# Probabilities turned on VectorE in 32-word squares instead of by transposing DMAs, and a causal mask added by products

## The chip, the cores and the metric

The kernel runs on one NeuronCore of one Trainium2 chip. Five engines work side by side from their own queues: TensorE (PE, with its weight loads PEld) multiplies matrices, VectorE (DVE) and ScalarE (ACT) work element by element, GpSimd (POOL) takes small side jobs and issues some DMAs, SyncE (SP) issues most DMAs. Sixteen DMA engines move the data. The metric is the device time of the program in microseconds (us); lower is better.

## The reference

One block of a transformer on a sequence of S = 2048 tokens of width 512: latent attention with 16 heads, a residual and a layer norm, then one linear layer, a residual and a layer norm.

```python
cq = rms_norm(x @ w_qa.T, q_a_ln_w)                       # 384 wide
q  = (cq @ w_qb.T) -> 16 heads of 128 (nope) + 64 (rope)
ckv = x @ w_kva.T                                         # 128 latent + 64 rope
kv = (rms_norm(ckv[..., :128], kv_a_ln_w) @ w_kvb.T) -> k_nope 128, v 128 per head
scores = (q_full @ k_full.T) * 192 ** -0.5
scores = where(causal, -inf, scores)
attn = softmax(scores)
out = (attn @ v) @ w_o.T
x = layernorm(x + out)
x = layernorm(x + x @ (weight * scale_weight[:, None]).T + bias)
```

## The kernel before

**Precision.** The products run at a precision of fp32 by splitting: a value is kept as a high and a low part (`split`, L61), and a product is the sum of high x high, high x low and low x high. The probabilities are split into two fp16 halves, and so are the latent values `V`.

**Absorbed weights.** The per-head key weights are multiplied into the query weights (L170), so that all 16 heads share one set of keys `Kn` (latent, 128 wide) and `Kp` (rope), and one set of values `V`. The value weights and the output weights are multiplied into `wvo` (L189), which acts on the attention's latent outputs at the end.

**Blocks and units.** The queries are four blocks `b` of 512. Within a block the loop runs over 8 pairs of heads `p` and four tiles `qt` of 128 queries. A *unit* is (b, p, qt): two heads `j`, each with nk = (4b + qt + 1) x 128 keys, so 128 to 512 in block 0 and 1664 to 2048 in block 3. Block 0 works on both heads at once (`pair_scores`, `pair_probs`), the others head by head (`head_scores`, `head_probs`).

**One head.** TensorE computes the scores into PSUM, five products per piece of up to 512 keys (L421). In the diagonal 128 columns the mask (-1e30 above the diagonal) is added: in block 0 and for the first head of a pair in block 3 by a sixth product, identity x mask (L423), elsewhere by VectorE on PSUM (L427). VectorE takes the maximum (L459) and forms the `bias` (L466, L468). ScalarE takes the exponentials and their sums (L474) into `pr`. VectorE forms `inv` (L484 to L487). ScalarE writes the high fp16 half of `pr * inv` (L495), VectorE the low half (L498), both into `hl`, high and low in separate rows. Then SP issues a transposing DMA (L502; L535 in block 0), which puts the keys on the partitions of the target: `PT` in block 0, a stretch of `ring` later.

**Order.** From block 1 on the instructions of TensorE and SP stand in the order in which the program writes them, in block 3 (from its second unit) those of VectorE and ScalarE too; the rest is ordered by a scheduler. `head_probs` of a head is a generator that `head_scores` of the next head drives, so the L498 of a head fall among the reductions of the next one, and its DMA behind the next head's `bias`. `values` (L540) multiplies the turned probabilities with `V` (L551), in two halves. `run_values(lag)` (L701) runs one half after each head once `lag` units wait; `lag` is 3 in blocks 1 and 2, and 2 in block 3, where the ring holds three units. So in block 3 the first half of unit n - 2 follows the scores of the first head of unit n. The result `ot` goes to DRAM by SP (`put_off` and `put_in`, L294 to L308). Projections of the next pair (`qn` L391, `pe` L347 to L376) are slipped in by `fill` (L562).

**Buffers.** In blocks 1, 2, 3 `hl` has 6, 4, 2 buffers and `pr` 4, 2, 2.

**Final stage.** Outputs come back from DRAM, are split (`latent`, L736) and multiplied with `wvo` into `acc` (`accumulate`, L766). `value_output` (L184) makes the `wvo` that are not there yet. Per tile of 128 tokens follow `residual`, `first_norm` and `ffn` (L867): transposes, split, GpSimd adds the bias to the residual (L874), 12 products (L880), VectorE adds both (L882), `layer_norm` (L847, whose root is two GpSimd instructions, L195 and L196), and one DMA out (L884).

Of the kernel before, what the change touches and what calls it, by code (L numbers as in the profile page):

```python
# [9 lines left out]
F16 = mybir.dt.float16  # L10
# [39 lines left out]
def mla_block(ctx: ExitStack, tc: tile.TileContext, a, out):  # L50
# [44 lines left out]

    ctx_kv = ctx.enter_context(ExitStack())
    kv = ctx_kv.enter_context(tc.tile_pool(name="kv", bufs=1))
    Kn = kv.tile([P, 2, S], F32R, name="Kn")
# [5 lines left out]
    with tc.tile_pool(name="ps_w", bufs=1, space=PSUM) as ps_w:  # L104
# [3 lines left out]
        for _ in range(10):  # L108
            nc.tensor.matmul(idle, ramp[:, :P], ramp, start=True, stop=True)

    blk = ctx.enter_context(tc.tile_pool(name="blk", bufs=2, side="right"))
    ctx_p = ctx.enter_context(ExitStack())
# [71 lines left out]
    def value_output(p, pool, tag):  # L184

        wvo = state["wvo"][p]
        for j in range(2):
            ps = pool.tile([P, HID], F32, tag=tag, name=f"ps_wo{2 * p + j}")
            nc.tensor.matmul(ps, state["wv"][:, 2 * p + j], state["wo"][2 * p + j], start=True, stop=True)  # L189
            split(ps, wvo[:, 0, j, :], wvo[:, 1, j, :], kvln_o)  # L190
            yield

    def rsqrt(dst, ms, n, eps):
        t = small.tile([P, 4], F32, tag="rs", name="rs_t")
        nc.gpsimd.tensor_scalar_add(t[:, :n], ms, eps)  # L195
        nc.gpsimd.tensor_tensor(dst, t[:, :n], nhalf[:, :n], ALU.pow)  # L196
# [212 lines left out]
    def score(ps, c0, w, b, p, j, qt, masked):  # L409

        qs = slice(qt * P, (qt + 1) * P)
        qn = state["qn", b, p]
        pe = state["pe", b, p // 2]
        qh, ql = qn[:, 0, j, qs], qn[:, 1, j, qs]
        qp = pe[:, 2 * (p % 2) + j, qs]

        by_product = b == 0 or b == 3 and j == 0
        ops = [(qh, Kn, 0), (qh, Kn, 1), (ql, Kn, 0), (qp, Kp, 0), (qp, Kp, 1)]
        n = 0
        for lhs, K, i in ops:  # L420
            nc.tensor.matmul(ps[:, :w], lhs, K[:, i, c0 : c0 + w], start=n == 0, stop=n == 4)  # L421
            if n == 1 and masked is not None and by_product:
                nc.tensor.matmul(ps[:, masked : masked + P], identb, maskb, start=False, stop=False)  # L423
            n += 1
        if masked is not None and not by_product:
            dg = ps[:, masked : masked + P]
            nc.vector.tensor_tensor(dg, dg, maskb, ALU.add)  # L427

# [3 lines left out]
    def head_scores(pools, b, p, j, qt, nk, prev):  # L432
# [36 lines left out]
        for _ in prev:  # L469
            pass  # L470
        pr = pools[1].tile([P, nk], F32, tag="pr", name=f"pr{b}_{p}_{qt}_{j}", bufs=4 if b == 1 else 2)
        sums = small.tile([P, 2], F32, tag="sums", name="sums")
# [15 lines left out]
        return pr, inv  # L488

    def head_probs(pools, b, p, j, qt, nk, PT, pr, inv):  # L490
        hl = pools[0].tile([P, 2, nk], F16, tag="hl", name=f"hl{b}_{p}_{qt}_{j}", bufs=(6, 4, 2)[b - 1])
        step = nk if nk <= 1024 else nk // 2
        cuts = [slice(c, c + step) for c in range(0, nk, step)]
        for c in cuts:
            nc.scalar.activation(hl[:, 0, c], pr[:, c], AF.Copy, scale=inv)  # L495
        yield
        for c in cuts:
            nc.vector.scalar_tensor_tensor(hl[:, 1, c], pr[:, c], inv, hl[:, 0, c], ALU.mult, ALU.subtract)  # L498
            if c != cuts[-1]:
                yield  # L500
        n2 = 2 * nk
        nc.sync.dma_start_transpose(  # L502
            PT[:, j * n2 : (j + 1) * n2].rearrange("p (k q) -> p k q", q=P), hl.rearrange("p a c -> p (a c)")
        )
        put_in()

    def pair_scores(pool, b, p, qt, nk):
# [3 lines left out]
        ps = psum["s"].tile([P, 2, 512], F32, tag="s", name=f"s{b}_{p}_{qt}")  # L511
        for j in range(2):
            score(ps[:, j, :], 0, w, b, p, j, qt, nk - P)
        neg = small.tile([P, 2], F32, tag="neg", name="neg")
# [14 lines left out]
    def pair_probs(pool, b, p, qt, nk, PT, pr, inv):  # L529
        hl = pool.tile([P, 2, 2, nk], F16, tag=f"hl{qt}", name=f"hl{b}_{p}_{qt}")  # L530
        for j in range(2):
            iv = inv[:, j : j + 1]
            nc.scalar.activation(hl[:, j, 0, :], pr[:, j, :], AF.Copy, scale=iv)
            nc.vector.scalar_tensor_tensor(hl[:, j, 1, :], pr[:, j, :], iv, hl[:, j, 0, :], ALU.mult, ALU.subtract)
        nc.sync.dma_start_transpose(  # L535
            PT[:, : 4 * nk].rearrange("p (k q) -> p k q", q=P), hl.rearrange("p j a c -> p (j a c)")
        )
        yield

    def values(b, p, qt, nk, PT):  # L540

        kts = nk // P
        v = PT[:, : 4 * nk].rearrange("p (j a k q) -> p j a k q", j=2, a=2, k=kts)
        ps = psum["m"].tile([P, 512], F32, tag="m", name=f"o{b}_{p}_{qt}")
# [296 lines left out]
    def load_fw(kt):  # L841
        raw = pc.tile([P, HID], F32, tag="xb", name=f"fraw{kt}", bufs=2)
        nc.scalar.dma_start(raw, a["fw"][:, kt])
        nc.vector.tensor_tensor(raw, raw, fsc, ALU.mult)
        split(raw, fw[:, 0, kt, :], fw[:, 1, kt, :])

    def layer_norm(dst, src):  # L847
        st = small.tile([P, 6], F32, tag="bn", name="bn")
        nc.vector.bn_stats(st, src)  # L849
        mv = small.tile([P, 2], F32, tag="mv", name="mv")  # L850
        nc.vector.bn_aggr(mv, st)
        r = small.tile([P, 1], F32, tag="lnr", name="lnr")
        rsqrt(r, mv[:, 1:2], 1, 1e-5)
        nc.vector.tensor_scalar(dst, src, mv[:, 0:1], r, ALU.subtract, ALU.mult)

# [11 lines left out]
    def ffn(t, x1):  # L867
# [5 lines left out]
        xb = pc.tile([P, HID], F32, tag="xb", name=f"xb{t}", bufs=2)  # L873
        nc.gpsimd.tensor_tensor(xb, x1, fb, ALU.add)  # L874
        yield 1
        ps = ps_f.tile([P, HID], F32, tag="ff", name=f"ff{t}")
        n = 0
        for kt in range(KT):
            for l, i in ((0, 0), (0, 1), (1, 0)):
                nc.tensor.matmul(ps, xt[:, l, kt, :], fw[:, i, kt, :], start=n == 0, stop=n == 11)  # L880
                n += 1
        nc.vector.tensor_tensor(xb, ps, xb, ALU.add)  # L882
        layer_norm(xb, xb)
        nc.sync.dma_start(out[0, t * P : (t + 1) * P, :], xb)  # L884

# [8 lines left out]
    with tc.manual_schedule(engines={ET.PE}):  # L894
        order = [(b, p) for b in range(NB) for p in range(NPAIR)]
        for b in range(NB):
            last = b == NB - 1
            if b:
                accs = [ps_a.tile([P, HID], F32, tag="acc", name=f"acc{b}_{t}") for t in range(4)]
            for p in range(0 if b else EARLY, CUT if last else NPAIR):  # L900
# [3 lines left out]
                for t in range(4):  # L904
                    accumulate(accs[t], p, t, *cuts[b, p])
                    if b == 0 and p + 2 < NPAIR and t == 1:
                        for _ in value_output(p + 2, ps_f, "ff"):
                            pass
                    if (p, t) in ((1, 2), (2, 0), (2, 2), (3, 0), (3, 2), (4, 0), (4, 2), (5, 0)):
                        advance()  # L910
# [76 lines left out]
```

## Time and profile before

| | us |
|---|---|
| median of 3 runs (lowest to highest) | 1588.22 (1586.73 to 1588.98) |
| the profiled execution, its time | 1588.17 |
| its span | 1586.40 |
| granted TensorE clock over the span | 0.993 |
| block 0's units, 52.2 to 253.6 of the span | 201.3 |
| block 1, 253.6 to 495.5 | 241.9 |
| block 2, 495.5 to 851.9 | 356.4 |
| block 3, 851.9 to 1331.7 | 479.8 |
| final stage, 1331.7 to 1586.4 | 254.7 |
| 192 transposing DMAs of blocks 1 to 3, issue to landing, median | 5.5 |

The span runs from the program's first profiled instruction to its last, and what lies around it is 1.77 us. A busy time is the time in which an engine has an instruction under way, and not a measure of how well it is used. In a group of instructions the columns are line, engine, operation, names of the output and the inputs, shapes, count, then busy us and the mean ns of one, then the idle time of the engine ahead of them and what ended it. A row of a timeline has start, length, engine, line, operation, names and the count of merged instructions; SPq is SP issuing a DMA. PE starts of successive products tell their pace, since the recorded lengths overlap.

### The profile page before, as it was taken

Reading aid. Unit: us, or ns where it says so; the run is one execution under the profiler, and the core shown is the slowest. Engines: PE = TensorE matmul, PEld = TensorE weight load, DVE = VectorE, ACT = ScalarE, POOL = GpSimd, SP = SyncE. Lnnn points to the kernel's source line nnn. Section 1 sums busy time; section 2 is a strip of 40 time slices with the busy share of each in tenths; the row PEclk is TensorE's granted clock in tenths of the full one; section 3 lists DMA queues with packets and bytes.
Section 4 is the critical chain, followed back from the end, with each engine's and each line's share of the span. In section 5 each row is a group of like instructions: output and inputs, shape, how many; then the busy total and the mean of one; then the engine's idle time right before and its main releaser. Section 6 shows DMA issues by size and latency. Waiting matters only on the chain. (4 is left out here: it accounts for less than half of the span.)

```text
span 1586.4 us, 24671 instructions
## 1 busy us (share of the span) xinstructions
PE 1546.3 (97%) x9130; PEld 1291.1 (81%) x9130; DVE 1161.2 (73%) x2099; ACT 924.7 (58%) x1631; POOL 361.5 (23%) x434
## 2 busy tenths in 40 slices
PE   8899998999999999999999999999999999999997
PEld 7688877888887788888888788888888886788886
DVE  6777777878787978787786877877777775465564
ACT  5767776665665676666765665665666665311120
POOL 2243325154016204050032401400400000022132
PEclk9999999999999999999999999999999999999999
DMA  7879877788897987788897888878678798433230
GB/s 230 258 197 240 191 191 160 147 176 190 149 218 163 173 163 165 159 162 170 160 204 148 168 145 168 156 143 165 140 143 176 148 233 196 146 118 122 94 113 33
DMA packets 633032, 262.49 MB, mean 165 GB/s; under 512 B 570288, under 2 KB 611376, under 8 KB 631888
## 3 DMA queue, kind: packets, MB, share of 16 engines
q1 hardware_dynamic: 621472, 233.62, 68.8%
q0 software_dynamic: 4672, 17.73, 3.6%
q10 hardware_dynamic: 6768, 9.57, 2.1%
q8 instruction: 72, 1.18, 0.3%
q14 instruction: 48, 0.39, 0.1%
HBM read 83.17 MB, written 35.13 MB: 75 GB/s over the span
## 5 line engine op out<-in xcount | busy, mean ns | idle before, releaser
L421 PE MATMUL s<-Kn,qn 128*128 128x512 f32 (+4 forms) x1920 | 521.1, 376 | 9.4 <-ACT pr L474 4.4
L474 ACT ACTIVATE pr<-s,bias,rq 128x1024 f32<-128x1024 f32 (+3 forms) x320 | 324.4, 1017 | 217.0 <-DVE bias L468 157.2
L498 DVE SCALAR_TENSOR_TENSOR hl<-pr,inv,hl 128x1024 f16<-128x1024 f32 (+7 forms) x320 | 359.6, 1137 | 38.7 <-ACT hl L495 34.9
L421 PEld LDWEIGHTS s<-Kn,qn 128*128 128x128 f32 x1920 | 339.5, 190 | 55.7 <-ACT pr L474 7.4
L551 PEld LDWEIGHTS <-V 128*128 128x128 f16 x3264 | 302.5, 98 | 86.6 <-issue 47.6
L551 PE MATMUL o<-ring,V 128*128 128x256 f16 x3024 | 362.9, 273 | 2.5 <-DVE qn L68 1.2
L421 PE MATMUL s<-Kp,pe 128*128 128x512 f32 (+4 forms) x1280 | 361.4, 363 | 0.0
L495 ACT ACTIVATE hl<-pr,inv 128x1024 f16<-128x1024 f32 (+7 forms) x320 | 294.6, 961 | 91.3 <-issue 34.5
L459 DVE TENSOR_REDUCE neg<-s 128x1 f32<-128x1024 f32 (+3 forms) x320 | 317.8, 993 | 38.0 <-PE s L421 34.9
L421 PEld LDWEIGHTS s<-Kp,pe 128*128 128x128 f32 x1280 | 234.0, 189 | 29.6
L359 POOL TENSOR_TENSOR prod<-prod 128x512 f32<-128x512 f32 x15 | 19.4, 1292 | 639.1 <-DVE prod L352 639.0
L391 PE MATMUL ps_qn<-cq,wq 128*128 128x512 f32 x576 | 145.1, 397 | 3.1 <-ACT ot L556 1.7
L770 PE MATMUL acc<-wvo,oh 128*128 128x512 f32 x448 | 143.9, 402 | 1.8 <-ACT pr L474 1.8
L374 POOL TENSOR_TENSOR pe<-prod,ph 32x512 fp32r<-32x512 f32 x92 | 138.8, 1509 | 6.0
L391 PEld LDWEIGHTS ps_qn<-cq,wq 128*128 128x128 f32 x576 | 107.3, 190 | 24.8 <-ACT ot L556 2.4
L770 PEld LDWEIGHTS acc<-wvo,oh 128*128 128x128 f32 x448 | 83.1, 188 | 23.2 <-issue 3.8
L486 DVE TENSOR_SCALAR inv<-sums 128x1 f32<-128x1 f32 x128 | 27.0, 211 | 97.5 <-ACT pr L474 97.5
L770 PE MATMUL acc<-wvo,ol 128*128 128x512 f32 x224 | 88.1, 393 | 0.0
L556 ACT ACTIVATE ot<-o 128x256 f32<-128x256 f32 x128 | 48.4, 378 | 45.2 <-PE o L551 39.6
L347 PE MATMUL ps_pe<-cq,wpe 128*128 128x512 f32 x288 | 73.8, 402 | 0.2 <-DMA cq<-cq_d 0.2
L64 ACT ACTIVATE oh<-o 128x1024 fp32r<-128x1024 f32 x28 | 29.7, 1060 | 65.6 <-PE acc L770 50.0
L65 DVE TENSOR_TENSOR ol<-o,oh 128x1024 fp32r<-128x1024 f32 x28 | 38.8, 1387 | 39.3 <-ACT oh L64 39.3
(147 smaller groups left out, 1631.6 us busy)
## 6 DMA issues: line engine op xcount, KB each, us to landing
wq<-wq_d SPq DMA_DIRECT2D x22, 768.0 KB, 5.7
o<-ot_d SPq DMA_DIRECT2D x32, 512.0 KB, 3.3
ot_d<-ot SPq DMA_DIRECT2D x97, 128.0 KB, 2.4
wpe<-wpe_d SPq DMA_DIRECT2D x10, 768.0 KB, 5.4
wq<-wq_d POOLq DMA_DIRECT2D x9, 768.0 KB, 6.4
cq_d<-cqst SPq DMA_DIRECT2D x18, 256.0 KB, 4.8
wo<-in_wo_dram SPq DMA_DIRECT2D x4, 1024.0 KB, 5.3
x<-in_x_dram SPq DMA_DIRECT2D x16, 256.0 KB, 3.7
```

Of the source, the lines that this page charges most:

```text
L65: nc.vector.tensor_tensor(l, ps, h.bitcast(F32), ALU.subtract)
L347: nc.tensor.matmul(ps, w[:, i, lt, x * P : (x + 1) * P], cq[:, k, lt, :], start=n == 0, stop=n == 8)
L374: (nc.gpsimd if not quick or (b, g) == (0, 0) and j % 2 else nc.vector).tensor_tensor(pe[64 + 32 * x : 96 + 32 * x, j, :], rp[q, x, :], ph ...
L391: nc.tensor.matmul(ps, w[:, i, lt, j * P : (j + 1) * P], cq[:, k, lt, :], start=n == 0, stop=n == 8)
L421: nc.tensor.matmul(ps[:, :w], lhs, K[:, i, c0 : c0 + w], start=n == 0, stop=n == 4)
L459: nc.vector.tensor_reduce(neg[:, ti : ti + 1], v, axis=AX.XY, op=ALU.max, negate=True)
L474: nc.scalar.activation(pr[:, c0 : c0 + n * w].rearrange("p (a c) -> p a c", a=n), v, AF.Exp, bias=bias, scale=r, accum_out=sums[:, ti : ti ...
L495: nc.scalar.activation(hl[:, 0, c], pr[:, c], AF.Copy, scale=inv)
L498: nc.vector.scalar_tensor_tensor(hl[:, 1, c], pr[:, c], inv, hl[:, 0, c], ALU.mult, ALU.subtract)
L551: nc.tensor.matmul(ps[:, :256], vt[:, i, k % 4, :], v[:, :, l, k, :], start=n == 0, stop=n == 3 * kts - 1)
L556: nc.scalar.activation(ot, ps[:, :256], AF.Copy)
L770: nc.tensor.matmul(acc, l[:, t, c], state["wvo"][p][:, i, j, :], start=p == 0 and j == 0 and n == 0, stop=p == NPAIR - 1 and j == 1 and n ...
```

## The change

- A head's two fp16 halves are written side by side, so that high and low half of one probability form one 32-bit word (`words`, `hl` being a strided view of it).
- `turn`: VectorE transposes the words in squares of 32 x 32, within each group of 32 partitions, into the buffer of `pr`, whose contents are no longer needed. SP then writes that to a DRAM tile `sq`. `gather`: after the second head of a pair, four DMAs, one per group of 32 target partitions, read the squares from DRAM to the partitions of their keys. In block 0 a pair is turned at once. `values` reads its operand with a step of one word.
- Buffers: `words` has 4, 3, 2 in blocks 1 to 3, `pr` 5, 3, 2; `sq` four per block.
- The mask is a product everywhere, the last of its group; in block 0 the two heads' masks come behind both heads' products.
- Final stage: value-output products are made for two pairs at a time, four products ahead of their splits; the identity is added to the second linear layer's weights, so the residual comes out of the product, and GpSimd's addition goes; in `layer_norm` the epsilon is added by VectorE; the products with the high part of `xt` come before those with the low part; for the last tile the bias is added by two products with one row, the scaling is done in halves, and each half is stored from its own queue (SP and ACT).
- Two small tiles shift the places of later ones in SBUF.

```diff
@@ score
-        by_product = b == 0 or b == 3 and j == 0
+        by_product = masked is not None
         ops = [(qh, Kn, 0), (qh, Kn, 1), (ql, Kn, 0), (qp, Kp, 0), (qp, Kp, 1)]
...
-            if n == 1 and masked is not None and by_product:
-                nc.tensor.matmul(ps[:, masked : masked + P], identb, maskb, start=False, stop=False)
...
-            nc.vector.tensor_tensor(dg, dg, maskb, ALU.add)
+        for n, (lhs, K, i) in enumerate(ops):
+            nc.tensor.matmul(ps[:, :w], lhs, K[:, i, c0 : c0 + w], start=n == 0, stop=n == 4 and not by_product)
+        def mask():
+            nc.tensor.matmul(ps[:, masked : masked + P], identb, maskb, start=False, stop=True)
+        if by_product:
+            if b == 0:
+                return mask
+            mask()
@@ head_scores
-        pr = pools[1].tile([P, nk], F32, tag="pr", name=f"pr{b}_{p}_{qt}_{j}", bufs=4 if b == 1 else 2)
+        pr = pools[1].tile([P, nk], F32, tag="pr", name=f"pr{b}_{p}_{qt}_{j}", bufs=(5, 3, 2)[b - 1])
@@ new
+    def turn(words, sq, dst):
+        nc.vector.transpose(
+            sq.rearrange("p (k c r) -> p c k r", k=4, r=32), words.rearrange("p (c k r) -> p c k r", k=4, r=32)
+        )
+        nc.sync.dma_start(dst, sq.rearrange("p (k x) -> p k x", k=4))
+    def gather(PT, src):
+        for k in range(4):
+            nc.sync.dma_start(
+                PT[32 * k : 32 * k + 32].bitcast(F32).rearrange("p (q x) -> p q x", q=4),
+                src[:, k].rearrange("(q p) x -> p q x", q=4),
+            )
@@ head_probs
-        hl = pools[0].tile([P, 2, nk], F16, tag="hl", name=f"hl{b}_{p}_{qt}_{j}", bufs=(6, 4, 2)[b - 1])
+        words = pools[0].tile([P, nk], F32, tag="hl", name=f"hl{b}_{p}_{qt}_{j}", bufs=(4, 3, 2)[b - 1])
+        hl = words.bitcast(F16).rearrange("p (n a) -> p a n", a=2)
...
-        nc.sync.dma_start_transpose(
-            PT[:, j * n2 : (j + 1) * n2].rearrange("p (k q) -> p k q", q=P), hl.rearrange("p a c -> p (a c)")
-        )
+        if j == 0:
+            state["sq"] = dram.tile([P, 4, nk // 2], F32, tag=f"sq{b}", name=f"sq{b}_{p}_{qt}", bufs=4)
+        sq = state["sq"]
+        turn(words, pr, sq[:, :, j * nk // 4 : (j + 1) * nk // 4])
+        if j == 1:
+            gather(PT, sq)
         put_in()
@@ pair_probs
-        nc.sync.dma_start_transpose(
-            PT[:, : 4 * nk].rearrange("p (k q) -> p k q", q=P), hl.rearrange("p j a c -> p (j a c)")
-        )
+        sq = dram.tile([P, 4, nk // 2], F32, tag="sq0", name=f"sq{b}_{p}_{qt}", bufs=4)
+        turn(words, pr.rearrange("p j n -> p (j n)"), sq)
+        gather(PT[:, : 4 * nk], sq)
@@ values
-        v = PT[:, : 4 * nk].rearrange("p (j a k q) -> p j a k q", j=2, a=2, k=kts)
+        v = PT[:, : 4 * nk].rearrange("p (q j k r a) -> p j a k q r", j=2, q=4, a=2, k=kts)
@@ load_fw
+        dg = raw[:, kt * P : (kt + 1) * P]
+        nc.vector.tensor_tensor(dg, dg, ident, ALU.add)
@@ layer_norm
-        rsqrt(r, mv[:, 1:2], 1, 1e-5)
-        nc.vector.tensor_scalar(dst, src, mv[:, 0:1], r, ALU.subtract, ALU.mult)
+        nc.vector.tensor_scalar(t, mv[:, 1:2], 1e-5, None, ALU.add)
+        nc.gpsimd.tensor_tensor(r, t, nhalf[:, :1], ALU.pow)
+        for i in range(parts):
+            c = slice(i * HID // parts, (i + 1) * HID // parts)
+            nc.vector.tensor_scalar(dst[:, c], src[:, c], mv[:, 0:1], r, ALU.subtract, ALU.mult)
@@ ffn
-        nc.gpsimd.tensor_tensor(xb, x1, fb, ALU.add)
+        if last:
+            one, fbr = state["fb"]
+            for i in range(2):
+                nc.tensor.matmul(ps, one, fbr[:, i, :], start=i == 0, stop=False)
+        ops = [(0, i, kt) for kt in range(KT) for i in range(2)] + [(1, 0, kt) for kt in range(KT)]
...
-        nc.vector.tensor_tensor(xb, ps, xb, ALU.add)
+        if not last:
+            nc.vector.tensor_tensor(xb, ps, fb, ALU.add)
+        layer_norm(xb, ps if last else xb, 2 if last else 1)
@@ final loop
-                    if b == 0 and p + 2 < NPAIR and t == 1:
-                        for _ in value_output(p + 2, ps_f, "ff"):
+                    if b == 0 and p % 2 == 0 and p + 2 < NPAIR and t == 1:
+                        value_outputs((p + 2, p + 3), ps_f, ("ff", "tp"))
```

## The prediction

> **What bounds the kernel now.** I read the busy times of the page first, then the same by stage (a table of windows, cut where the first score reduction of each block of 512 queries starts), then the groups by line, and last the timeline of one unit of work (a head pair at one tile of 128 queries).
>
> ```profile
> PE 1546.3 (97%) x9130; PEld 1291.1 (81%) x9130; DVE 1161.2 (73%) x2099; ACT 924.7 (58%) x1631; POOL 361.5 (23%) x434
> ```
>
> TensorE is busy 97% of the span. By stage (us; the columns are PE, PEld, DVE, ACT, POOL, granted clock, DMA share, GB/s; the rows are blocks 1, 2, 3 and the final stage):
>
> ```profile
> 253.60:495.50 241.90, 239.09 (x1440) 202.80 (x1439) 194.78 (x415) 153.61 (x242) 81.65 (x72) 0.99 0.85 175
> 495.50:851.90 356.40, 353.76 (x2151) 298.05 (x2150) 291.64 (x543) 240.53 (x434) 83.16 (x72) 1.00 0.84 167
> 851.90:1331.70 479.80, 474.79 (x2894) 393.38 (x2893) 358.11 (x515) 302.03 (x442) 65.29 (x56) 1.00 0.80 159
> 1331.70:1586.40 254.70, 244.99 (x1126) 196.26 (x1124) 130.66 (x196) 52.87 (x65) 49.72 (x80) 0.99 0.36 116
> ```
>
> In blocks 1 to 3 TensorE idles 1%, so nothing that the other engines do delays it; the 25% that the page's mean leaves to VectorE is only 18 to 25% in the blocks that the change touches. Block 0 (52.2 to 253.6) has PE 189.7 and DVE 155.0 of 201.3 us.
>
> **The turn on VectorE.** Added: one transpose of nk words per head in blocks 1 to 3 (192), of 2nk words per pair in block 0 (32). A block's 16 heads carry 128 x (5+6+7+8) x 16 = 53,248 words per partition in block 1, 86,016 in block 2, 118,784 in block 3, 20,480 in block 0. No row shows a VectorE transpose. The nearest rows have one input and one element out or in per step:
>
> ```profile
> L459 DVE TENSOR_REDUCE neg<-s 128x1 f32<-128x1024 f32 x144 | 175.4, 1218 | 35.8 <-PE s L421 34.9
> L459 DVE TENSOR_REDUCE neg<-s 128x1 f32<-128x384 f32 x32 | 17.7, 553 | 0.2
> L854 DVE TENSOR_SCALAR x<-x,mv,lnr 128x512 f32<-128x512 f32 x16 | 8.7, 542 | 5.6 <-POOL lnr L196 5.3
> ```
>
> The two reductions give (1218 - 553) / 640 = 1.04 ns per element and 0.15 us fixed. The fastest fp32 row, L854, gives (542 - 150) / 512 = 0.77 ns. From above, the L498 products that run beside GpSimd take a median 1.91 us for 896, 1.96 ns per element. I take 1.04, because the slopes of L459 and of an undisturbed L498 (1.28 us for 1024) agree; fixed 0.19 us a turn (0.15, and 0.04 for the wait on L498's result, the gap that dependent VectorE instructions show). [...]
>
> Removed from VectorE: the 160 mask additions of L427 (46.8 us; 18.5, 18.6 and 9.4 in blocks 1, 2, 3). VectorE's work becomes
>
> - block 1: 194.8 - 18.5 + 55.5 + 12.1 = 243.9 of today's 241.9 us
> - block 2: 291.6 - 18.6 + 89.6 + 12.1 = 374.7 of 356.4
> - block 3: 358.1 - 9.4 + 123.8 + 12.2 = 484.7 of 479.8
> - block 0: 155.0 + 21.3 + 6.1 = 182.4 of 201.3
>
> So VectorE's cover is gone: in three blocks it has more work than the block lasts today. The strided halves of hl cost ScalarE and VectorE nothing here: their rows already run at one element per step. TensorE then reads the halves at a 4-byte step, as far apart as the fp32 operands it takes at full rate (231 ns for 512 columns, against 109 for 256 of fp16); I take nothing; at the fp32 rate per column (0.451 against 0.426 ns) the 3264 value products would take 21 us more, and nothing in the rows speaks for a gain.
>
> **The mask as a product.** 160 products are added. The trace prices one where block 3 has it today:
>
> ```profile
> 1154.97 0.23 PE L423 MATMUL s<-maskb,identb 128*128 128x128 bf16 x1
> ...
> 1155.01 0.39 PE L421 MATMUL s<-Kn,qn 128*128 128x320 f32 x1
> ...
> 1155.24 0.31 PE L421 MATMUL s<-Kp,pe 128*128 128x320 f32 x1
> ```
>
> From the mask's start to the second product behind it pass 0.27 us; one product of 320 columns takes 0.147 from start to start, so the mask adds 0.123 (0.119 to 0.127 over all shapes). That is 8.0, 8.0 and 3.9 us, and TensorE's work becomes 247.1, 361.8 and 478.7. This is the floor under any good outcome. Behind fp16 value products the switch could be partly shared: from 0.04 to 0.13.
>
> **The longer way to the values.** Removed: 224 transposing DMAs. Added: 224 writes of the words to DRAM, and per pair four reads, which SP issues only when the second write has landed. The engines' load hardly changes. A head of block 3 (mean nk 1856) today moves 3712 packets of 256 bytes, 23 ns mean, on 16 engines: 5.4 us. Now it writes 512 packets of nk bytes and reads 256 of 2nk. Packet medians in the trace are 46 ns for 1024 bytes, 84 for 2048, 159 for 4096, hence 77 and 145 ns, 2.5 + 2.3 us. SP issues 6 short DMAs (0.33 to 0.57 us each) per pair where it now issues two of 3 to 5 us; its loads and the `ot` stores stand behind the wait for the write, and have several us to spare.
>
> [...]
>
> What changes is latency. In block 3 the way is this (the last unit of the fifth head pair, nk 2048; the SP row merges two issues, of which the first is this unit's):
>
> ```profile
> 1158.07 1.28 DVE L498 SCALAR_TENSOR_TENSOR hl<-pr,inv,hl 128x1024 f16<-128x1024 f32 x1
> ...
> 1159.37 10.00 SPq L502 DMA_TRANSPOSE ring<-hl  x2
> ...
> 1168.50 1.70 PE L551 MATMUL o<-ring,V 128*128 128x256 f16 x14
> ```
>
> L498 ends at 1159.35, the transpose is issued and lands at 1167.66, the value product that reads it starts at 1168.50: 0.8 us to spare. Over the block's 32 units the spare time (landing to first use) is 0.8 to 9.2, mean 5.5 us; in block 2 7 to 20, mean 13.3; in block 1 0 to 19, mean 6.2; in block 0 often 0 to 5.
>
> Per unit of block 3 the way grows by: 0.6 (`inv` now stands behind the turn on VectorE, which ends about 3.3 us after `bias`, while the exponentials end at 2.7) + 2.1 (turn) + 4.5 (write: 2.5 of packets and the 2.0 that a small store needs beyond its packets) + 6.9 (read of both heads: 4.6, 2.0, and 0.3 for four issues) - 6.7 (today's mean landing) = 7.4 us. With lag 2 the values of a unit stand three heads' work behind its last scores. A head lasts 7.50 us now, so the way is 3 x 7.50 - 5.5 = 17.0 us; it becomes 24.4, and a head can't be shorter than 24.4 / 3 = 8.13 us. Block 3: 64 x 8.13 = 520, **+41**. That exceeds VectorE's 484.7. `pr`, two buffers there, is now held until the write lands, some 8 us behind the previous `bias`: just inside this head.
>
> Block 2: the way grows by some 5.5 us, inside its 13. VectorE sets it: 374.7, and with 3% lost to waits, since TensorE is 97% loaded beside it, 386: **+30**. Block 1: TensorE 247.1 and VectorE 243.9 together, the way 4.6 longer with 6.2 spare but uneven; at 97% 255: **+13**. Block 0: 182.4 fits, but several units have no spare time: **+6**, between 0 and 15.
>
> **The final stage** is TensorE's (245 of 254.7). The value-output products move in groups of four, unchanged in number; the identity folded into the weights adds four VectorE additions of 0.3 us and drops 16 GpSimd additions of 1.4 us, both beside products; the bias row is two products placed ahead of the last tile's wait. Only the end is on the path: one VectorE addition less (0.69 + gap), the last scaling in halves (0.25), the fp32 low parts later (0.7 us seen before the third product of the last tile). **-2**, at most -4.
>
> **Sum.** 6 + 13 + 30 + 41 - 2 = +88. The profiled execution took 1588.17 (span 1586.40 and 1.77 around it), 0.05 below the median 1588.22: **1676 us**.
>
> **Rivals.** (a) The latency is covered and the turn is cheap (0.77 ns a word): VectorE falls to 230, 352 and 453, TensorE decides with its masks: 20 - 2 = +18, 1606. With VectorE alone deciding at 97%, block 3 at 500, it is 1655. For: most DMAs can start earlier, as SP is free. Against: block 3's 0.8 to 2 us spare in its longest units. Chance 0.22 for 1606 to 1645.
> (b) The DMAs land later under load (packets of 6144 bytes have a mean of 325 ns beside a median of 234): data terms 30% longer make block 3's head 8.8 us (+85), and 92% use of VectorE gives +51 in block 2, +23 in block 1, +15 in block 0: 1760. Chance 0.15 for 1710 to 1760.
> (c) The turn costs twice as much, like L498 beside GpSimd: VectorE 293, 453 and 593, over 1840. Chance 0.07.
> (d) The other side: the turn stays under about 0.8 us for 1024 words, so VectorE keeps below 94% of TensorE's new work everywhere, and the freed SP and DMA engines end TensorE's waits: at most its 11.6 us idle in block 0 and 10.4 in blocks 1 to 3, and 2 at the end, against 20 of masks: 1584. For: the DMA share reaches 0.99 between 100 and 150 us. Against: both conditions are needed, and the waits of TensorE name few DMAs (2.0 and 0.5 us). Chance 0.08.
>
> **Numbers.** The forecast, 1645 to 1710, has 0.48. The range 1606 to 1760 holds (a), the forecast and (b), 0.85. What a measurement tells from no change is some 0.2%, 3 us. Faster 0.05, same 0.03, slower 0.92.
>
> **What would show it.** Right: a VectorE transpose near 1.2 us for 1024 words; VectorE over 93% in block 2; TensorE waiting before the value products for the `ring` reads in block 3, the write landing near 4.5 and the reads near 7 us. Wrong: VectorE idle in block 2, TensorE still at 99% in blocks 1 to 3, or the turn outside 0.9 to 1.5 us per 1024 words.

## The result and the profile after

The changed kernel takes 1967.97 us (median of 4 runs, 1958.08 to 1974.24) beside 1588.6 for the kernel before on the same chip: 1.238 times as long, 95% interval 1.232 to 1.245. The forecast was 1676, the range 1606 to 1760: slower, as forecast, but by 379 us where 88 were expected.

The page of the changed kernel: busy times, the granted clock in 40 slices, DMA traffic, and two lines of the chain that ended last (by engine, then by line; it could be followed back to 879 us of the span).

```profile
PE 1661.1 (84%) x9292; PEld 1343.5 (68%) x9292; DVE 1442.4 (73%) x2200; ACT 998.9 (51%) x1633; POOL 334.1 (17%) x386
...
PEclk9999989988999999999989989998999898899999
...
DMA packets 248672, 405.20 MB, mean 205 GB/s; under 512 B 21952, under 2 KB 179008, under 8 KB 247520
...
PE 20%; DMA 16%; DVE 13%; ACT 4%; issue 2%; SPq 1%; ACTq 0%; POOLq 0%; POOL 0%; DVEq 0%
DMA sq<-pr 11%; PE acc L803 8%; DVE hl L528 5%; DVE pr L506 4%; PE o L584 4%; DMA ring<-sq 4%; PE s L431 4%; DVE neg L472 3%; ACT pr L487 2%; PE ff L924 2%; ACT hl L525 2%; PE ps_qn L403 1%; SPq L514 1%; DMA o<-ot_d 0%; PE ps_wo L201 0%
```

VectorE's share is 73% as before, and TensorE's fell from 97 to 84%: now no engine is full. The chain says why: its largest entry is a DMA, the write of the turned words (`sq<-pr`, 11%), with their reads (`ring<-sq`) at 4%. The same by stage (the columns are PE, PEld, DVE, ACT, POOL, granted clock, DMA share, GB/s; the rows are blocks 1, 2, 3 and the final stage):

```profile
285.70:609.20 323.50, 268.29 (x1511) 219.66 (x1511) 242.42 (x416) 166.50 (x242) 81.00 (x72) 0.91 0.74 208
609.20:1071.20 462.00, 388.88 (x2227) 312.09 (x2225) 372.49 (x543) 260.69 (x434) 84.01 (x72) 0.96 0.81 223
1071.20:1701.50 630.30, 513.84 (x2909) 406.62 (x2908) 485.07 (x546) 335.31 (x441) 64.90 (x56) 0.92 0.79 216
1701.50:1972.50 271.00, 247.83 (x1126) 197.10 (x1124) 133.57 (x234) 54.67 (x68) 20.89 (x32) 0.96 0.39 124
```

VectorE's busy time is what the prediction worked out (242.4, 372.5, 485.1 us for 243.9, 374.7, 484.7), yet the blocks last 324, 462 and 630 us. TensorE is busy longer than the added work explains (513.8 us in block 3, 478.7 worked out), at a lower granted clock (0.92 there, 1.00 before). What TensorE, VectorE and ScalarE wait for most, over the whole span (us in total, times, longest; GpSimd's waits are left out):

```profile
ACT pr L487 <- DMA sq<-pr: 216.7, 58, 12.0
PEld L584 <- issue: 184.2, 117, 9.0
PE o L584 <- DMA ring<-sq: 147.5, 41, 8.8
DVE inv L499 <- ACT pr L487: 119.7, 43, 10.0
ACT ot L589 <- DMA ot_d<-ot: 118.6, 38, 6.5
ACT hl L525 <- DVE inv L500: 95.4, 96, 4.1
```

Three of the six name DMAs, and SP issues all three kinds: ScalarE waits to overwrite `pr` until it has been written to DRAM, TensorE for the reads, ScalarE again for the old `ot` to be stored. One unit of block 3 shows how they meet:

```profile
1400.90 1.75 SPq L514 DMA_DIRECT2D ring<-sq  x4
...
1402.85 1.91 DVE L506 STREAM_TRANSPOSE pr<-hl 128x1664 f32<-128x1664 f32 x1
...
1404.82 0.52 SPq L509 DMA_DIRECT2D sq<-pr  x1
...
1413.23 3.15 PE L584 MATMUL o<-ring,V 128*128 128x256 f16 x14 [5.51 <-DMA ring<-sq]
...
1415.23 1.20 ACT L487 ACTIVATE pr<-s,bias,rq 128x1024 f32<-128x1024 f32 x1 [3.27 <-DMA sq<-pr]
```

SP issues the four reads at 1400.90. By the trace's landing times they land one after the other, at 1405.92, 1408.29, 1410.74 and 1413.10, and 0.13 us later the value product starts that waited 5.51 us. The next head's write is issued at 1404.82, lands behind all four reads at 1415.12, and only then may ScalarE write the next exponentials. The longer way to the values thus becomes a wait of TensorE, and through the write that lands behind the reads a wait of ScalarE too.

### The profile page after: what moved, and what is told of

It is laid out like the page before. It is cut to its first block, busy times and chain, and to the rows that moved or that the text cites. A ratio compares the mean times of both kernels' runs of the same rounds, so it can differ in the third digit from the quotient of the medians.

```text
span 1972.5 us, 25934 instructions
## 1 busy us (share of the span) xinstructions
PE 1661.1 (84%) x9292; PEld 1343.5 (68%) x9292; DVE 1442.4 (73%) x2200; ACT 998.9 (51%) x1633; POOL 334.1 (17%) x386
## 2 busy tenths in 40 slices
DMA packets 248672, 405.20 MB, mean 205 GB/s; under 512 B 21952, under 2 KB 179008, under 8 KB 247520
## 4 chain that ended last, share of the span: by engine, by line
PE 20%; DMA 16%; DVE 13%; ACT 4%; issue 2%; SPq 1%; ACTq 0%; POOLq 0%; POOL 0%; DVEq 0%
DMA sq<-pr 11%; PE acc L803 8%; DVE hl L528 5%; DVE pr L506 4%; PE o L584 4%; DMA ring<-sq 4%; PE s L431 4%; DVE neg L472 3%; ACT pr L487 2%; PE ff L924 2%; ACT hl L525 2%; PE ps_qn L403 1%; SPq L514 1%; DMA o<-ot_d 0%; PE ps_wo L201 0%
## 5 line engine op out<-in xcount | busy, mean ns | idle before, releaser
L431 PE MATMUL s<-Kn,qn 128*128 128x512 f32 (+4 forms) x1920 | 533.8, 387 | 86.3 <-ACT pr L487 73.9
L584 PE MATMUL o<-ring,V 128*128 128x256 f16 x3024 | 407.1, 289 | 177.9 <-DMA ring<-sq 147.5
L584 PEld LDWEIGHTS <-V 128*128 128x128 f16 x3264 | 317.1, 101 | 293.9 <-issue 184.2
L431 PEld LDWEIGHTS s<-Kn,qn 128*128 128x128 f32 x1920 | 351.5, 199 | 149.4 <-ACT pr L487 91.6
L528 DVE SCALAR_TENSOR_TENSOR hl<-pr,inv,hl 128x1024 f16<-128x1024 f32 (+7 forms) x320 | 390.8, 1236 | 72.6 <-ACT hl L525 72.4
L525 ACT ACTIVATE hl<-pr,inv 128x1024 f16<-128x1024 f32 (+7 forms) x320 | 363.1, 1197 | 96.7 <-DVE inv L500 95.4
L431 PE MATMUL s<-Kp,pe 128*128 128x512 f32 (+4 forms) x1280 | 374.0, 374 | 0.0
L506 DVE STREAM_TRANSPOSE pr<-hl 128x256 f32<-128x256 f32 (+6 forms) x224 | 328.7, 1469 | 2.8
L431 PEld LDWEIGHTS s<-Kp,pe 128*128 128x128 f32 x1280 | 245.0, 198 | 31.8
L385 POOL CAST pe<-prod 32x512 fp32r<-32x512 f32 x88 | 67.1, 763 | 3.3
```

What stands on the lines that cost most here:

```text
L385: nc.gpsimd.tensor_copy(to, rp[q, x, :])
L506: nc.vector.transpose(sq.rearrange("p (k c r) -> p c k r", k=4, r=32), words.rearrange("p (c k r) -> p c k r", k=4, r=32))
L584: nc.tensor.matmul(ps[:, :256], vt[:, i, k % 4, :], v[:, :, l, k, :], start=n == 0, stop=n == 3 * kts - 1)
```

## The experiments

**Theories.** (W) The way decides: the copies through DRAM take longer than assumed and hold `ring`, `pr` and `ot`. (V) VectorE's added turn decides, by disturbing the order beside a full TensorE. (H) The strided halves or a slower clock decide. The recorded expectations use letters of their own, which they explain. Times by stage, us, cut at the first score reduction of each block (block 0 from its own first; the final stage from some 6 us behind the last score reduction), one profiled execution each; each ratio is against the kernel before, run beside it:

| kernel | block 0 | block 1 | block 2 | block 3 | final | median | ratio (95%) |
|---|---|---|---|---|---|---|---|
| before | 201 | 242 | 356 | 480 | 254 | 1588.2 | 1 |
| after | 231 | 324 | 462 | 630 | 271 | 1968.0 | 1.238 (1.232 to 1.245) |
| x1_dmat | 205 | 242 | 362 | 477 | 255 | 1597.6 | 1.005 (1.004 to 1.007) |
| x3_turn | 206 | 259 | 426 | 504 | 260 | 1710.1 | 1.076 (1.073 to 1.079) |
| x9_noturn | 218 | 315 | 423 | 594 | 260 | 1865.5 | 1.174 (1.170 to 1.177) |
| x2_wide | 220 | 314 | 443 | 587 | 265 | 1887.6 | 1.188 (1.185 to 1.190) |
| x6_fixed | 215 | 290 | 453 | 620 | 268 | 1910.9 | 1.202 (1.199 to 1.206) |
| x14_wide_fixed | 211 | 279 | 430 | 566 | 266 | 1819.5 | 1.145 (1.143 to 1.147) |
| x17_noturn_wf | 199 | 249 | 366 | 504 | 255 | 1635.8 | 1.030 (1.027 to 1.033) |
| x16_wfps | 209 | 277 | 391 | 547 | 261 | 1749.5 | 1.101 (1.098 to 1.105) |
| x4_rows | 226 | 317 | 456 | 622 | 268 | 1944.8 | 1.224 (1.221 to 1.226) |
| x5_pool | 248 | 353 | 461 | 644 | 272 | 2038.0 | 1.282 (1.278 to 1.286) |
| x8_pr3 | 229 | 323 | 442 | 627 | 262 | 1935.3 | 1.218 (1.213 to 1.223) |
| x12_store | 231 | 313 | 463 | 631 | 271 | 1960.9 | 1.234 (1.232 to 1.236) |
| x11_lag5 | 225 | 323 | 470 | 649 | 270 | 1989.6 | 1.252 (1.250 to 1.255) |
| x15_lag5_store | 231 | 309 | 471 | 645 | 271 | 1983.2 | 1.248 (1.245 to 1.252) |
| x18_ot | 226 | 319 | 470 | 628 | 269 | 1966.9 | 1.238 (1.235 to 1.241) |
| x19_ot_lag5_store | 225 | 307 | 462 | 642 | 269 | 1961.9 | 1.236 (1.234 to 1.238) |
| x20_wf_ot | 211 | 261 | 422 | 568 | 266 | 1792.1 | 1.128 (1.126 to 1.130) |
| x13_best | 199 | 242 | 357 | 482 | 256 | 1592.5 | 1.002 (1.001 to 1.003) |

**x1_dmat**, the change without its turn and copies, with the halves in separate rows and the buffer counts of the kernel before:

```diff
-        words = pools[0].tile([P, nk], F32, ...)
-        hl = words.bitcast(F16).rearrange("p (n a) -> p a n", a=2)
+        hl = pools[0].tile([P, 2, nk], F16, ...)
...
-        turn(words, pr, sq[...])
-        if j == 1: gather(PT, sq)
+        nc.sync.dma_start_transpose(PT[...], hl.rearrange("p a c -> p (a c)"))
```

> The changed kernel with the transposing DMAs, the halves in separate rows and the old buffer counts put back; the mask products, the final stage and the rest of the change stay. Theory A (the reads into 32 partitions run at half rate and hold the queue): all of the loss lies in the turn and its copies, so this run is near the kernel before plus the masks, 1588 + 20 - 2 = 1590 to 1610 us. Theory B (VectorE's load and the latency of two DRAM passes, at any rate of the reads): the same, 1590 to 1610. Theory C (the mask products and the new order of the final stage cost more than their rows say, by slowing the granted clock): over 1640 us.

Masks as products and the new final stage cost 9 us together. The rest, some 370 us, lies in what x1 puts back: the turn, the copies, and the strided halves and buffer counts that go with them.

**x3_turn**, the kernel before with VectorE's transposes as work alone, whose result nobody reads:

```diff
+        turn(hl.rearrange("p a c -> p (a c)").bitcast(F32), pr)
```

> The kernel before with the VectorE transposes added as work alone: each turns the fp16 rows, taken as words, into pr, behind the issue of the transposing DMA, and nothing reads the result. The masks stay on VectorE as before. VectorE's work becomes 262, 393 and 494 us in blocks 1 to 3, against 242, 356 and 480 us that they last. Theory B: 1660 to 1710 us, since VectorE becomes the bound with some waits. Theory A allows the same but holds that this is the smaller part of the 380 us. If VectorE's load is absorbed, 1590 to 1620 us.

+122 us; block 2 is the surprise, 426 us. Its row of the windows (columns as above):

```profile
521.80:947.40 425.60, 380.17 (x2180) 313.58 (x2179) 380.36 (x611) 240.26 (x436) 81.31 (x72) 0.95 0.70 141
```

TensorE and VectorE are each busy 380 us of 426, 89%. VectorE's work is a little under the 393 us expected; the 97% use was not to be had, with the two `pr` of the kernel before (the changed kernel has three there). ScalarE now waits for the turn to leave `pr`, and for VectorE's `inv`:

```profile
ACT pr L474 <- DVE pr L492: 40.2, 13, 4.3
ACT pr L474 <- DVE inv L487: 37.5, 13, 4.4
```

**x9_noturn**, the other half: the copies without the turn.

```diff
-        nc.vector.transpose(...)
-        nc.sync.dma_start(dst, sq.rearrange("p (k x) -> p k x", k=4))
+        nc.sync.dma_start(dst, words.rearrange("p (k x) -> p k x", k=4))
```

> The changed kernel without VectorE's transposes: the words are written to DRAM as they stand and read as before. It leaves out the turn inside each group, so the output is not the reference's. The turn alone, added to the kernel before, took 122 us. If the parts add up: 1968 - 122 = 1830 to 1860 us. Theory P (turn, write and the next exponentials are one loop through pr; here words is held in place of pr): 1750 to 1830 us. If the copies were hidden without VectorE's load: under 1650 us.

+268 us over x1, just above the 1830 to 1860 us expected if the parts add. They nearly do: 1598 + 122 + 268 = 1988, measured 1968. Taken so, the copies are two thirds of the loss, (W); the turn a third, (V). The split is not fixed, as x14 and x17 below show.

**What in the copies: x2_wide, x6_fixed, x14_wide_fixed.** x2 moves the same bytes in four reads of the same packet sizes, but each read goes to all 128 partitions instead of 32. x6 reads a fixed place in DRAM, so that no read waits for a write. x14 does both. Packets (248672) and bytes of x2 are those of the changed kernel.

```diff
         for k in range(4):
-            nc.sync.dma_start(PT[32 * k : 32 * k + 32]..., src[:, k].rearrange("(q p) x -> p q x", q=4))
+            nc.sync.dma_start(PT.bitcast(F32)[:, k * w : (k + 1) * w], src[:, k])       # x2
+            nc.sync.dma_start(PT[32 * k : 32 * k + 32]..., fixed[:, k, ...])             # x6
+            nc.sync.dma_start(PT.bitcast(F32)[:, k * w : (k + 1) * w], fixed[:, k, :w])  # x14
```

> The changed kernel with each of the four reads taking one quarter of the columns to all 128 partitions instead of all columns to 32 partitions; packets of the same number and size, the same waits. It leaves out the exchange between the groups of 32 partitions, so the output is not the reference's. Theory A: the packets of 3328 bytes fall from a median 255 to some 131 ns, four reads land within 7 us instead of 12, and the time falls to 1680 to 1740 us. Theory B: the latency of a write and a read in series and VectorE's load stay, 1930 to 1980 us. Theory D (the strided halves): 1930 to 1980 us.

> The changed kernel with its reads taking the same bytes from a fixed DRAM tile, so they don't wait for the write; turn, writes and packets stay. The values are multiplied with constant numbers, so the output is not the reference's. Theory L (the write and the reads in series are too late for the values): TensorE's waits before the value products fall from 178 us to under 60 us, the time to 1830 to 1900 us. Theory P (pr): the value products wait less, but ScalarE's waits for sq<-pr stay and the time stays within 1920 to 1970 us.

> The changed kernel with reads of quarter columns to all 128 partitions, taken from a fixed DRAM tile: the half rate and the wait for the write are both gone; the turn, the writes and all bytes stay. It leaves out the exchange between partition groups and multiplies the values with constants, so the output is not the reference's. If these two are all that the copies cost, what is left is the turn and the masks, 1598 + 122 = 1720, with the strided halves 1740 us. If SP's order and the buffers pr and ot hold the rest: 1790 to 1840 us.

They give back 80, 57 and 148 us. x2 and x6 gave less than their theories of the reads asked for (1680 to 1740 and 1830 to 1900 us): neither the rate nor the wait is the whole. x14 came within the 1790 to 1840 us expected if SP's order and the buffers hold the rest. The issues (KB each, median us from issue to landing), of the stores before, then of the changed kernel, then of x2:

```profile
ot_d<-ot SPq DMA_DIRECT2D x97, 128.0 KB, 2.4
```

```profile
sq<-pr SPq DMA_DIRECT2D x16, 832.0 KB, 9.8
ring<-sq SPq DMA_DIRECT2D x32, 416.0 KB, 6.8
ot_d<-ot SPq DMA_DIRECT2D x97, 128.0 KB, 6.4
```

```profile
sq<-pr SPq DMA_DIRECT2D x16, 832.0 KB, 6.9
ring<-sq SPq DMA_DIRECT2D x32, 416.0 KB, 4.7
ot_d<-ot SPq DMA_DIRECT2D x97, 128.0 KB, 5.1
```

A packet of 3328 bytes takes a median 255 ns into 32 partitions in the changed kernel. That is 1.95 times the 131 that x2's expectation has for all 128, an estimate between the 84 ns of 2048 bytes and the 159 of 4096 in the kernel before. In x2 the packets of the queue that carries the reads (q1) take 59.0% of the 16 engines' span, 67.0% in the changed kernel, and the reads of 416 KB land after 4.7 us instead of 6.8. The writes of 832 KB come home earlier too, after 6.9 us instead of 9.8, and the `ot` stores after 5.1 instead of 6.4. Why a read into 32 partitions takes longer was not shown.

**x17_noturn_wf**, x14 without the turn.

> The run with wide reads from a fixed tile without VectorE's transposes; the words are written as they stand. It leaves out the turn and uses constants for the values, so the output is not the reference's. If the half rate and the wait for the write are all that the copies cost: 1600 to 1640 us. If the writes and the queue still cost by themselves: 1680 to 1740 us.

1636, so without the turn all but 38 of the copies' 268 us come from these two, the rate into 32 partitions and the wait of the reads for the write. With the turn they give back 148 only: x14 less x17 makes the turn 184 us, where alone it cost 122.

**x8_pr3 and x16_wfps.** x8 gives `pr` a buffer more in blocks 2 and 3, at the cost of `words`; x16 adds that to x14, and the stores of x12.

```diff
-        pr = ... bufs=(5, 3, 2)[b - 1]
+        pr = ... bufs=(5, 4, 3)[b - 1]
-        words = ... bufs=(4, 3, 2)[b - 1]
+        words = ... bufs=(4, 2, 1)[b - 1]
```

> The changed kernel with pr in 5, 4, 3 buffers and words in 4, 2, 1 in blocks 1 to 3 (the same SBUF in block 3). Theory P: ScalarE's waits for sq<-pr fall from 217 us to under 40 us, and the time to 1850 to 1900 us. Theory L: those waits go, but TensorE waits for the reads instead, and the time stays within 1930 to 1980 us.

> The run with wide reads from a fixed tile (1819 us), with pr in 5, 4, 3 and words in 4, 2, 1 buffers, and the ot stores ahead of the reads. Data as in that run, so the output is not the reference's. Theory P (what is left above turn and masks is pr held until the write lands, and the stores): 1720 to 1760 us, block 3 from 566 to 500 to 525 us. If the load of the DMA engines or VectorE's longer way sets it: 1790 to 1820 us.

Alone, the buffer gives 33 us, 20 of them in block 2 and only 3 in block 3: ScalarE's wait for `sq<-pr` falls from 217 to 6 us, and others stand in its place (the first row names nothing; in block 3 VectorE's `bias` ends 0.085 us before most of these starts):

```profile
ACT pr L487 <- issue: 182.1, 64, 8.3
...
ACT ot L589 <- DMA ot_d<-ot: 153.4, 41, 8.7
PE o L584 <- DMA ring<-sq: 142.5, 37, 8.0
```

Beside the faster reads it gives, with the stores, 70; block 3 is at 547, above the 500 to 525 expected. Block 2 is then at 391 us, close to the forecast's 386, with VectorE busy 368.5 us, 94%: its high use was possible, with one more `pr` and reads that are quick and wait for no write.

**x4_rows** writes high and low halves into separate rows again, so that a turned word pairs neighbouring keys instead of the halves of one probability.

```diff
-        hl = words.bitcast(F16).rearrange("p (n a) -> p a n", a=2)
+        hl = words.bitcast(F16).rearrange("p (a n) -> p a n", a=2)
```

> The changed kernel with the high and the low halves in separate rows of the same buffer, as in the kernel before, so that no write has a step of two; turn, write and reads move the same bytes. A word then holds two neighbouring keys instead of the two halves of one, so the output is not the reference's. Theory D (strided halves cost 0.3 ns per element on ScalarE and 0.15 on VectorE, some 100 us of busy time): ScalarE's 1024-column copy falls from 1.44 to 1.14 us, VectorE's product from 1.43 to 1.28 us, and the time falls to 1870 to 1900 us. Theory A: the durations fall so, but the time falls by 10 to 30 us only, since the DMA queue sets the pace.

Of the halves of 1024 elements, VectorE's (L528) and ScalarE's (L525), in the changed kernel and then in x4:

```profile
L528 DVE SCALAR_TENSOR_TENSOR hl<-pr,inv,hl 128x1024 f16<-128x1024 f32 x48 | 68.5, 1434 | 12.1 <-ACT hl L525 12.1
L525 ACT ACTIVATE hl<-pr,inv 128x1024 f16<-128x1024 f32 x48 | 66.9, 1443 | 14.4 <-DVE inv L500 14.4
```

```profile
L528 DVE SCALAR_TENSOR_TENSOR hl<-pr,inv,hl 128x1024 f16<-128x1024 f32 x48 | 62.0, 1297 | 6.3 <-ACT hl L525 6.3
L525 ACT ACTIVATE hl<-pr,inv 128x1024 f16<-128x1024 f32 x48 | 53.1, 1142 | 12.9 <-DVE inv L500 12.8
```

The step costs VectorE 0.13 and ScalarE 0.29 ns per element, and the kernel 23 us. Real, and small: this part of (H) is not the cause.

**x5_pool** lets GpSimd issue the reads instead of SP, in a queue of their own.

```diff
-            nc.sync.dma_start(PT[32 * k : 32 * k + 32]...
+            nc.gpsimd.dma_start(PT[32 * k : 32 * k + 32]...
```

> The changed kernel with its four reads per pair issued by GpSimd instead of SP; SP keeps the writes, the stores and the loads, and no longer waits for a write to land. Theory Q (the queue: while SP waits for a write, and while reads lie ahead in its queue, the next write and the ot stores stand behind, which holds pr and ot): ScalarE's 217 us of waits for sq<-pr and 119 us for ot_d<-ot fall below half, and the time falls to 1780 to 1880 us. Theory P (pr is held by the turn and the write themselves, wherever the reads are issued): 1920 to 1980 us.

Worse, 2038, outside both ranges. The reads' wait for the write now holds GpSimd, and TensorE waits longer for the reads (147.5 us before this edit):

```profile
POOL ring L514 <- DMA sq<-pr: 794.8, 63, 21.3
...
ACT pr L487 <- DMA sq<-pr: 215.4, 46, 10.3
PE o L584 <- DMA ring<-sq: 214.2, 46, 16.8
```

The `ot` stores, no longer behind the reads, land after 4.4 us instead of 6.4, and ScalarE's 119 us of waits for them are gone. Its waits for `sq<-pr` stay: in block 3 the first head's write still takes a mean 7.9 us (8.3 in the changed kernel). So the order in SP's queue holds the stores, but is not all that makes the writes late.

**Block 1: x11, x12, x15, x18, x19, x20.** Its 324 us were the least understood. x11 lets the values come five units late instead of three (in block 1 alone), x12 issues the `ot` stores ahead of the reads, x15 does both; x18 has six `ot` buffers in block 1, x19 all three, x20 all three on top of x14.

```diff
-        lag = min(ring.shape[1] // (2048 * (b + 1)) - 1, 3) if b else 2
+        lag = min(ring.shape[1] // (2048 * (b + 1)) - 1, 5) if b else 2     # x11, x15, x19, x20
...
+        put_in()                                                           # x12, x15, x19, x20
         if j == 1:
             gather(PT, sq)
-        put_in()
...
-        ot = blk.tile([P, 256], F32, tag="ot", ...)
+        ot = (pools[0] if b == 1 else blk).tile(..., bufs=6 if b == 1 else 2)   # x18, x19, x20
```

> The changed kernel with lag 5 instead of 3 in block 1, so that a unit's values stand nine heads behind its last scores instead of five; blocks 0, 2 and 3 as they are. Theory L (the way through DRAM, late for the values, sets block 1): block 1 falls from 323 to 265 to 285 us, near the 259 that it took with the turn alone. Theory S (SP waits, the ot stores behind the reads hold ScalarE, the writes hold pr): block 1 stays within 310 to 330 us, and the whole within 1950 to 1980 us.

> The changed kernel with SP issuing the waiting ot store between the second write of a pair and its four reads, instead of behind the reads, so it no longer stands behind SP's wait for the write nor behind the reads in the queue. Theory S: ScalarE's 119 us of waits for ot_d<-ot fall below 40 us, and the time falls to 1880 to 1930 us, most of it in blocks 1 and 2. Theory L: the waits go, the time stays within 1940 to 1980 us.

> The changed kernel with lag 5 in block 1 and the ot stores ahead of the reads. Theory S+L (in block 1 two waits stand behind each other, the values' for the reads and ScalarE's for the ot buffer, so that taking one away shows the other): block 1 falls from 323 to 265 to 290 us, while lag alone left it at 323 and the store order at 313. If VectorE's order or the writes hold it: 305 to 315 us.

> The changed kernel with six buffers instead of two for the attention results ot, in block 1 alone. In block 1 ScalarE waits 50.0 us for ot stores (17 times, up to 6.5 us), the longest of its waits there, and the scores behind it in ScalarE's queue wait with it. If that paces block 1, it falls from 323.5 us to 275-295 and the kernel to 1918-1940. If the wait is only where a slow way shows itself (VectorE's and the ring's waits take its place), block 1 stays above 310 and the kernel above 1955.

> The same with a lag of five units in block 1 and the ot stores issued ahead of the reads (in all blocks). Neither the ring nor ot can hold block 1 then: if these two paced it, it comes near the 259 us that it has with the turns alone, say 255-280, and the kernel takes 1905-1935. If VectorE and ScalarE waiting for each other pace it, it stays above 300.

> The last one with the reads spread over all partitions and taken from a fixed place, without a wait for the write; it leaves out that the values read the right probabilities. Block 1 had 278.7 us with these two and no ot buffers. If ot and the pr held by the write are what is left, block 1 comes to 255-265; if not, it stays at 275-280. The other blocks should be near those of the kernel with the two edits alone (430, 566), less some 5-20 us for the earlier stores.

With the longer lag the reads of x11 have a mean 17.7 us to spare in block 1 (6.6 at the least), and it lasts as long as before. x12 ends ScalarE's waits for `ot` stores (119 us to 3), but those for `sq<-pr` rise from 217 to 241, and the kernel gains 7. Without the `ot` wait in block 1 (50 us there, x18) the block takes 319. With all three it is still 307, and ScalarE now waits there for the writes (x19, block 1):

```profile
ACT pr L487 <- DMA sq<-pr: 68.6, 22, 8.7
```

Only with the reads quick as well does it fall, to 261, what the turn alone gives (x3: 259). The row of x20:

```profile
273.00:533.80 260.80, 242.45 (x1457) 197.95 (x1456) 240.50 (x417) 165.01 (x240) 84.53 (x72) 0.98 0.81 262
```

So no single buffer paces block 1. The slow reads sit under `ring`, `ot` and `pr`; whichever is given room, the next is late. x11, x15, x18 and x19 stayed above the ranges in which a buffer would have paced the block.

**x13_best**, the kernel before with the new final stage and the mask as a product in all of block 3: 1592.5, where 1583 to 1587 was expected.

```diff
-        by_product = b == 0 or b == 3 and j == 0
+        by_product = b in (0, 3)
```

> The kernel before with the change's final stage and its buffer padding, and the mask as a product for both heads in block 3 only (blocks 1 and 2 on VectorE, block 0 in place, as before); transposing DMAs stay. Block 3 took 3.5 us less with all masks as products, and the end behind the last product 0.8 us less: 1583 to 1587 us, 0.1 to 0.3% below the kernel before. Theory C (the final stage's order costs as much as it saves): 1587 to 1592 us.

Block 3 +2, final stage +1.5: neither this choice of the change's other parts nor all of them (x1) beats the kernel before.

## Why the prediction was wrong in size

- **The turn, right.** 2312 ns for 2048 words and 1237 for 1024: 1.05 ns a word and 0.16 us, for 1.04 and 0.19.

```profile
L506 DVE STREAM_TRANSPOSE pr<-hl 128x2048 f32<-128x2048 f32 x16 | 37.0, 2312 | 0.6
...
L506 DVE STREAM_TRANSPOSE pr<-hl 128x1024 f32<-128x1024 f32 x24 | 29.7, 1237 | 0.0
```

- **Where the miss lies.** The profiled execution is 386 us longer, for 88: by block 30 for 6, 82 for 13, 106 for 30 and 150 for 41, and 16 for -2 in the final stage.
- **The way's reads, wrong: this is the step that failed.** "Read of both heads 6.9" took packets of 145 ns, from rows whose DMAs spread over all partitions; into 32 partitions the packets of 3840 bytes take 298. In block 3 the landing times give 2.2 us from the end of the second L528 to the write's issue (2.1 forecast for the turn), 5.2 to its landing (4.5), and 11.3 from the first read's issue to the last landing (6.9). The way grows by 2.2 + 5.2 + 11.3 - 6.7 + 0.6 = 12.6 us, not 7.4. Put into the forecast's own formula this makes (17.0 + 12.6) / 3 = 9.87 us a head; measured are 630.3 / 64 = 9.85. The reads' 4.4 us alone are 94 of the 110 us that block 3 lacked. The formula also meets x9 (9.15 for 9.28, without the turn) and x8, whose third `pr` does not help block 3 (9.74 for 9.80). It falls short of x2 (8.55 for 9.17) and x6 (9.34 for 9.69, by its 17.1 us from the second L528 to the last landing), where the way no longer decides alone; the 0.6 was not measured.
- **"Its loads and the `ot` stores ... have several us to spare": wrong.** An `ot` store lands after 6.4 us (2.4 before), and ScalarE waits 119 us for it; in block 3 the first head's write, which mostly comes behind another unit's reads, lands after a mean 8.3 us, the second's after 5.2. `pr`, "just inside this head", makes ScalarE wait 149 us in block 3.
- **VectorE's 97% use in block 2, wrong without a further `pr`, and the way there too.** The turn alone made 426 us of the forecast's 386, the copies alone 423 (x9); with four `pr` and quick reads it is 391. That 386 was a limit of VectorE's, and I had costed nothing for `pr` being held through turn and write there. From the second L528 to the last landing pass a mean 16.0 us, where the transposes landed after 5.6: 10.4 more, not 5.5, with 7 to 20 to spare.
- **Block 1's +13, wrong by the same way.** Its VectorE part, +17 in x3, is about right; the rest of +82 is the copies, whose way there is 9.3 us longer (13.8 for 4.5), not 4.6, with 6.2 to spare.
- **Strided halves "cost nothing", wrong and small:** 23 us by x4. TensorE reading them "I take nothing": successive value products start 113 ns apart (109 before), times 3264 is 13 us, inside the 21 that I bounded.
- **Masks, too dear:** with the final stage +9 (x1) for +18. In block 3, where the additions on VectorE go, the block even fell by some 3. The final stage was about +1 in x1, not -2. Its +16 in the changed kernel is late values of block 3: the last value product ends 46.6 us behind the start of the last score reduction, 30.3 before.
- **Rival (b), late DMAs under load,** was the right mechanism at the wrong price: it made the data terms 30% longer, where the reads' packets were twice as long as assumed (298 ns for 145), and reached 1760. It did not ask how many partitions a DMA lands in.
- **Two readings** were slightly off, with nothing resting on them: the page's mean leaves VectorE 27%, not 25, and the packets of 6144 bytes have a mean of 328 ns.

## What to carry to other kernels

Price a DMA from a row with the same number of partitions at its SBUF end, not only the same packet size: here packets of 3840 bytes into 32 partitions took 298 ns, and 145 were forecast. When a detour is added to a queue, follow every transfer that stands behind it to the buffer it frees: here taking away one wait showed the next (33 us from x8, 7 from x12), and taking the slow transfer away helped most (148 from x14). Before an engine is forecast at 97% beside another full one, count the buffers between them: VectorE had 89% of block 2 with two `pr` (x3), and 94% with four and quick reads (x16).

## What the runs showed that was not expected

In the changed kernel the granted clock falls in or behind most long waits of TensorE. The records have it at half in stretches that last 3.4 to 17.1 us there: 19 us in all in x1, 86 in x3, 254 in the changed kernel. From block 0 on, 33 of the changed kernel's 37 waits of TensorE over 3 us have such a stretch begin 2.2 to 5.3 us behind their start; of the 25 waits of 1 to 2 us 1 has one within 7. Inside these stretches successive value products start 213 ns apart, outside 113. TensorE is busy 105 us longer in the changed kernel than in x1 (1661.1 for 1556.1) with the same count of products (9292). Its busy time inside such stretches is 171 us, 13 in x1; half of the difference, 79, and the 13 of the strided halves would explain most of the 105, an estimate. For (H) this means little: on the chain that ended last, followed back to 879 us, TensorE's part has 42 us at half clock, so the clock itself cost that chain some 21 us, an estimate too. No run here holds the clock and keeps the waits, so its exact price stays open.
